# Cross-attention block: row sums of two units turned together, second exchange targets, and a changed order of work

## The chip, the cores and the metric

The kernel runs on one core of a Trainium2 chip. The metric is device time in microseconds (us), the median of several runs. A core has five engines with queues of their own: TensorE (PE, matrix products and transposes through the array), VectorE (DVE), ScalarE (ACT), GpSimd (POOL) and SyncE (SP, here only a queue that issues DMAs). Each engine works through its instructions in the order in which the program emits them, and waits where an operand or a buffer isn't ready.

## The reference

For four batches of 512 rows of width 512 (16 heads of 32):

```python
x = layer_norm(hidden_states, ln1_w, ln1_b)
q, k, v = x @ q_w + q_b, enc @ k_w + k_b, enc @ v_w + v_b     # split into heads
attn = softmax(where(mask, q @ k.T * scale, min))
hidden = (attn @ v) @ cproj_w + cproj_b + hidden_states
y = layer_norm(hidden, ln2_w, ln2_b)
y = gelu(y @ fc_w + fc_b)                                     # width 2048
return hidden + y @ proj_w + proj_b
```

All is float32.

## The kernel before

**Units and pairs.** Heads go in groups of four: w = 4 * batch + group, 16 in all. Each w has four units qt of 128 queries; unit u = 4w + qt runs from 0 to 63. Two units make a pair, number 2w + half, 0 to 31.

`scores` (L198) makes on PE the scores of one unit for four heads into one PSUM tile `sc`, of which there is a single buffer. DVE then adds the mask and finds each row's extreme (L210), and ACT takes the exponent and the row sum (L214), head by head. `turn` (L218) has to bring the 128 x 512 exponents of each head to a layout with keys on the partitions. For pairs 0, 3 and 6 (`ON_PE`) PE transposes them (`tpp`, L228) and DVE and ACT copy them out. For all others DVE transposes blocks of 32 x 32 into a tile `tb` (L242), and when the pair's second unit is done, 16 DMAs on SP's queue exchange the partition blocks from `tb` to a tile `pT` (L257). `tb` has two buffers, `pT` one. Two instructions of DVE in each unit bring the reciprocals of the row sums along: a reciprocal that is spread over 32 columns for each head (L245, `rrq`) and a transpose into the end of `tb` (L246). For a pair turned by PE, `over_sums` (L260) makes the spread reciprocals `rr` of both units at once, and `turn_sums` (L269) turns them on PE into `rb`.

`attend` (L279) multiplies a pair's turned exponents with v on PE (`av`, L299); DVE multiplies by the reciprocals into `oT` (L304), which is the last reader of `pT`. `cproj` (L323), `ln2` (L331), `ln2_turn`, `fc` (L355) and `proj` (L371) follow when a batch's eight pairs are done. `fc` writes gelu values to `gT`, four chunks for each quarter of the MLP, two buffers; `proj` reads them. The inputs of the projections are `encT` (L127) and `xT` (L149), one buffer each: encoder rows and normed rows, both with features on the partitions. `load_hid` (L315) fetches the residual and has POOL add a bias row; `ln2` norms each tile of it on DVE (L106) and has POOL add the MLP's output bias (L340), and `proj` adds its sums to it.

**Order.** Nothing is scheduled by a tool; each engine's order is the order of the calls. The main loop (L496) takes the units in turn: `scores`, then `attend` of the pair that is LAG = 4 units back (at even u, pair (u - 4) / 2), then `turn`. Between them it works off the list `first[w]`, and from qt = 2 on also `later[w]`, each item with a cost: 3.4 for a chain of PE, 0.5 for a set of four transposes, 0 for what doesn't use PE. A quarter of the sum is due in each unit, half of it before `turn` and half after (L513 to L519), and an item is taken while half its cost fits the budget (L423).

The lists are filled by hand (L457 to L493). A(w) loads the next weights and makes k, q and v; x1 to x4 load, take the statistics of, norm, turn and load the inputs of the next batch; C are the cproj chains, t2 the four turns of ln2, FC and PJ the chains of `fc` and `proj`, lo and hi the loads of the residual. For batch b at w = 4b:

```python
later[w] = C(p)
first[w + 1] = do(lambda: ln2(p))
first[w] = [load, ka] + x2[:1] + [qa] + x2[1:2] + p3[:1] + lo + x2[2:] + p3[1:3] + x3[:2] + [va] + x3[2:] + x4 + hi
first[w + 1] += [load, qa, ka] + t2[:2] + [va] + t2[2:] + p3[3:]
```

where p is the batch before. The last four items of PJ, FC and so on come after the loop (L522 on), with `attend` of pairs 30 and 31 between them.

Of the kernel before, what the change touches and what calls it, by code (L numbers as in the profile page):

```python
# [26 lines left out]
F32 = mybir.dt.float32  # L27
# [19 lines left out]
NW = B * NG  # L47
AHEAD = 3
LAG = 4
ON_PE = (0, 3, 6)  # L50
WARM = 14
PW = 2 * NT * HG * HD
# [7 lines left out]
def xattn_block(ctx: ExitStack, tc: tile.TileContext, x, encT, mask, q_w, k_w, v_w, c_w, fc_w, p_w, vecs, rows, out):  # L60
# [19 lines left out]
    nhalf = const.tile([P, NT], F32, tag="nhalf", name="nhalf")  # L80
    qb = const.tile([P, NG], F32, tag="qb", name="qb")
    wc = const.tile([P, ND, D], F32, tag="wc", name="wc")

    S = {}

# [37 lines left out]
    def queue(b):  # L123
        return nc.gpsimd if b else nc.sync

    def load_enc(b):
        S["eT", b] = one.tile([P, ND, L], F32, tag="encT", name=f"encT_{b}")  # L127
        for d in range(ND):
            queue(b).dma_start(out=S["eT", b][:, d, :], in_=encT[b, ts(d, P), :])

    def load_x(b):
        S["xn", b] = [tiles.tile([P, D], F32, tag="xn", name=f"xn1_{b}_{t}") for t in range(NT)]
# [12 lines left out]
            ln_rs((1, b))  # L145

    def ln1_turn(b, d):
        if d == 0:
            S["xT", b] = one.tile([P, ND, L], F32, tag="xT", name=f"xT_{b}")  # L149
        ln_turn((1, b), d, S["xn", b], S["xT", b])  # L150

    def make_mb(b):
        mb = one.tile([P, L], F32, tag="mb", name=f"mb_{b}")
# [11 lines left out]
    def prep_k(w):  # L165
        b, g = divmod(w, NG)
        kT = kqp.tile([P, L], F32, tag="kT", name=f"kT_{w}")
        acc = acc_tile(f"acck_{w}")
        for d in range(ND):
            nc.tensor.matmul(acc, S["wk", w][:, d, :], S["eT", b][:, d, :], start=(d == 0), stop=(d == ND - 1))  # L170
        nc.scalar.activation(kT, acc, AF.Identity, bias=vec[:, KB + g : KB + g + 1], scale=1.0)
        S["kT", w] = kT

    def prep_q(w):
        b, g = divmod(w, NG)
        qT = kqp.tile([P, L], F32, tag="qT", name=f"qT_{w}")
        acc = acc_tile(f"accq_{w}")
        for d in range(ND):
            nc.tensor.matmul(acc, S["wq", w][:, d, :], S["xT", b][:, d, :], start=(d == 0), stop=(d == ND - 1))  # L179

        nc.scalar.activation(qT, acc, AF.Identity, bias=qb[:, g : g + 1], scale=-scale)
        S["qT", w] = qT

    def prep_v(w):
        b = w // NG
        v = five.tile([P, NT, P], F32, tag="v", name=f"v_{w}")
        acc = acc_tile(f"accv_{w}")
        for t in range(NT):
            for d in range(ND):
                nc.tensor.matmul(  # L190
                    acc[:, ts(t, P)], S["eT", b][:, d, ts(t, P)], S["wv", w][:, d, :],
                    start=(d == 0), stop=(d == ND - 1),
                )
        nc.scalar.copy(v, acc.rearrange("p (t f) -> p t f", t=NT))
        S["v", w] = v
# [22 lines left out]
    def turn(w, qt):  # L218

        half, q = divmod(qt, 2)  # L220
        if 2 * w + half in ON_PE:
            if q == 0:

                S["pT", w, half] = two.tile([P, 2, NT, HG, P], F32, tag="tb", name=f"pT_{w}_{half}")
            for h in range(HG):
                tp = acc_tile(f"tpp_{w}_{qt}_{h}")
                for t in range(NT):
                    nc.tensor.transpose(tp[:, ts(t, P)], S["ps", w, qt][h][:, ts(t, P)], ident)  # L228
                o = S["pT", w, half][:, q, :, h, :]
                if h % 2:  # L230
                    nc.vector.tensor_copy(o, tp.rearrange("p (t q) -> p t q", t=NT))
                else:
                    nc.scalar.copy(o, tp.rearrange("p (t q) -> p t q", t=NT))
            return
        if q == 0:


            S["tb", w, half] = two.tile([P, NI, PW + 2 * HD], F32, tag="tb", name=f"tb_{w}_{half}")
        tb = S["tb", w, half]
        tv = tb[:, :, :PW].rearrange("p j (a t h q) -> p a h t j q", a=2, t=NT, h=HG)  # L240
        for h in range(HG):
            nc.vector.transpose(tv[:, q, h], S["ps", w, qt][h])  # L242

        rr = two.tile([P, HG, HD], F32, tag="rrq", name=f"rrq_{w}_{qt}")
        nc.vector.reciprocal(rr, S["sums", w][:, qt, :, None].broadcast_to([P, HG, HD]))  # L245
        nc.vector.transpose(tb[:, :, PW + q * HD : PW + (q + 1) * HD], rr.rearrange("p h d -> p (h d)"))  # L246
        if q == 0:
            return

        pT = one.tile([P, NI, PW + 2 * HD], F32, tag="pT", name=f"pT_{w}_{half}")  # L250

        for d in range(NI):
            for i in (0, 2, 1, 3):
                j = (i + d) % NI

                q = nc.scalar if w == NW - 1 and half and i % 2 else nc.sync
                q.dma_start(out=pT[ts(j, HD), i], in_=tb[ts(i, HD), j])  # L257
        S["pT", w, half] = pT

    def over_sums(w, half):  # L260

        if 2 * w + half not in ON_PE:
            return
        rr = one.tile([P, 2 * HG, HD], F32, tag="rr", name=f"rr_{w}_{half}")
        sums = S["sums", w][:, 2 * half : 2 * half + 2, :].rearrange("p t h -> p (t h)")
        nc.vector.reciprocal(rr, sums[:, :, None].broadcast_to([P, 2 * HG, HD]))
        S["rr", w, half] = rr.rearrange("p a d -> p (a d)")

    def turn_sums(w, half):  # L269
        if 2 * w + half not in ON_PE:  # L270
# [60 lines left out]
    def ln2(b):  # L331
        for f in range(FQ - 1):
            load_fc(b, f)
        ln_rs((2, b))
        S["yn", b] = [tiles.tile([P, D], F32, tag="xn", name=f"xn2_{b}_{t}") for t in range(NT)]
        for t in range(NT):
            h = S["hid", b, t]
            ln_norm((2, b), t, S["yn", b][t], h)

            nc.gpsimd.tensor_tensor(h, h, row[:, 1, :], ALU.add)  # L340

    def ln2_turn(b, d):
# [12 lines left out]
    def fc(b, f):  # L355
        q, k = divmod(f, FQ)

        if f + FQ - 1 < NF:
            load_fc(b, f + FQ - 1)
        if k == 0:  # L360
            S["gT", b, q] = two.tile([P, FQ, L], F32, tag="gT", name=f"gT_{b}_{q}")
        acc = acc_tile(f"accf_{b}_{f}")
        for d in range(ND):
            nc.tensor.matmul(acc, S["fw", b, f][:, d, :], S["yT", b][:, d, :], start=(d == 0), stop=(d == ND - 1))  # L364
        nc.scalar.activation(  # L365
            S["gT", b, q][:, k, :], acc, AF.Gelu_apprx_tanh, bias=vec[:, FCB + f : FCB + f + 1], scale=1.0
        )
        if q == 0:
            load_p(b, f)

    def proj(b, q, t):  # L371
        acc = acc_tile(f"accp_{b}_{q}_{t}")
        for k in range(FQ):
            nc.tensor.matmul(  # L374
                acc, S["gT", b, q][:, k, ts(t, P)], S["pw", b, q * FQ + k], start=(k == 0), stop=(k == FQ - 1)
            )
        h = S["hid", b, t]
        nc.vector.tensor_tensor(h, acc, h, ALU.add)  # L378
        if q == NQ - 1:
            nc.sync.dma_start(out=out[b, ts(t, P), :], in_=h)  # L380
        elif t == NT - 1:
            for k in range(FQ):
                load_p(b, (q + 1) * FQ + k)
# [5 lines left out]
    def do(fn):  # L389
        return [(0.0, fn)]  # L390
# [76 lines left out]
    for b in range(1, B):  # L467
        w = b * NG
        p = b - 1
        x1, x2, x3, x4 = inputs(b + 1) if b + 1 < B else ([], [], [], [])  # L470
        lo, hi = (do(lambda p=p, r=r: load_hid(p, r)) for r in ((0, 1), (2, 3)))
        p3 = PJ(b - 2, 3) if b > 1 else []
        t2 = turns2(p)
        first[w - (1 if b == 1 else 2)] += x1
        if b > 1:
            first[w - 1] += lo
            lo = []
        load, ka, qa, va = A(w + AHEAD)
        later[w] = C(p)
        first[w + 1] = do(lambda p=p: ln2(p))  # L480
        if b + 1 < B:
            first[w] = [load, ka] + x2[:1] + [qa] + x2[1:2] + p3[:1] + lo + x2[2:] + p3[1:3] + x3[:2] + [va] + x3[2:] + x4 + hi
            load, ka, qa, va = A(w + 1 + AHEAD)
            first[w + 1] += [load, qa, ka] + t2[:2] + [va] + t2[2:] + p3[3:]
        else:
            first[w] = [load, ka] + p3[:2] + hi
            first[w + 1] += [qa, p3[2]] + t2[:2] + [p3[3]] + t2[2:] + [va]
        first[w + 1] += FC(p, 0) + FC(p, 1)
        first[w + 2] = A(w + 2 + AHEAD) + PJ(p, 0) + FC(p, 2)
        f3 = FC(p, 3)  # L490
        first[w + 3] = A(w + 3 + AHEAD) + PJ(p, 1) + f3[:2]
        if b + 1 < B:
            first[w + 3] += PJ(p, 2) + f3[2:]  # L493

    nc.gpsimd.dma_start(out=wc, in_=c_w)
    for w in range(NW):  # L496
# [4 lines left out]
        due = 0.0  # L501
        for qt in range(NT):
            u = w * NT + qt
            at = divmod((u - LAG) // 2, 2) if u >= LAG and u % 2 == 0 else None
            if at:
                turn_sums(*at)
            scores(w, qt)
            if at:
                attend(*at)

            if qt == 2:
                work, rest = work + rest, []
# [20 lines left out]
    run(C(b))  # L533
    ln2(b)
    run(p3[2:])
    run(turns2(b))
    f3 = FC(b, 3)
    run(FC(b, 0) + FC(b, 1) + PJ(b, 0) + FC(b, 2) + PJ(b, 1) + f3[:2] + PJ(b, 2) + f3[2:] + PJ(b, 3))

# [43 lines left out]
```

## Time and profile before

| | |
|---|---|
| Time, median of 3 runs | 888.35 us (887.52 to 892.28) |
| The profiled run's own time | 889.65 us |
| Span of its instructions | 887.9 us |
| PE, busy | 849.1 us, 96% |
| DVE, busy | 511.6 us, 58% |
| ACT, busy | 337.1 us, 38% |
| POOL, busy | 167.4 us, 19% |
| Mean granted clock of TensorE | 0.983 |
| Exchanges pT<-tb | 456 DMAs on SP and 8 on ACT, 136 KB each, 2.5 us to landing |

A row of the groups reads: line, engine, operation, what it writes and reads, shape, number | busy us, mean ns of one | idle time of the engine just before, and what ended it. A line of the timeline reads: start in us, length in us, engine, line, operation, number in brackets after x, and in square brackets the idle time before it and who ended it. The granted clock is the share of its full rate that TensorE was given in a stretch. Durations come from the profiled run, the median from all runs.

### The profile page before, as it was taken

Reading aid. Unit: us, or ns where it says so; the run is one execution under the profiler, and the core shown is the slowest. Engines: PE = TensorE matmul, PEld = TensorE weight load, DVE = VectorE, ACT = ScalarE, POOL = GpSimd, SP = SyncE. Lnnn points to the kernel's source line nnn. Section 1 sums busy time; section 2 is a strip of 40 time slices with the busy share of each in tenths; the row PEclk is TensorE's granted clock in tenths of the full one; section 3 lists DMA queues with packets and bytes.
Section 4 is the critical chain, followed back from the end, with each engine's and each line's share of the span. In section 5 each row is a group of like instructions: output and inputs, shape, how many; then the busy total and the mean of one; then the engine's idle time right before and its main releaser. Section 6 shows DMA issues by size and latency. Waiting matters only on the chain.

```text
span 887.9 us, 10985 instructions
## 1 busy us (share of the span) xinstructions
PE 849.1 (96%) x3722; PEld 407.2 (46%) x3722; DVE 511.6 (58%) x1105; ACT 337.1 (38%) x699; POOL 167.4 (19%) x269
## 2 busy tenths in 40 slices
PE   9977979799999999999999999999999989999998
PEld 6535536445454544455454454435444334444443
DVE  3697757888547455778556635698567841501111
ACT  2646335334643434434453525424546320020000
POOL 2211001234101211224111110223101102521110
PEclk9998889899999999999999999999999999999999
DMA  7356265576854926566763835665757674232121
GB/s 262 107 134 171 66 152 147 134 207 161 207 149 109 264 67 172 156 175 181 203 167 79 220 98 125 165 188 148 199 123 194 153 172 144 83 118 82 43 80 56
DMA packets 43832, 130.14 MB, mean 147 GB/s; under 512 B 11456, under 2 KB 11456, under 8 KB 43648
## 3 DMA queue, kind: packets, MB, share of 16 engines
q1 hardware_dynamic: 26064, 71.40, 32.6%
q0 software_dynamic: 17184, 56.90, 21.5%
q10 hardware_dynamic: 528, 1.14, 0.6%
q8 instruction: 30, 0.49, 0.2%
q14 instruction: 26, 0.21, 0.1%
HBM read 60.58 MB, written 4.19 MB: 73 GB/s over the span
## 4 chain that ended last, share of the span: by engine, by line
PE 77%; DVE 8%; DMA 8%; SPq 4%; issue 1%; ACT 1%; POOL 0%; DVEq 0%; ACTq 0%
PE accp L374 23%; PE accf L364 21%; DMA pT<-tb 7%; PE av L299 6%; PE accv L190 6%; PE accq L179 6%; PE sc L205 5%; PE acck L170 5%; SPq L257 4%; DVE s L210 3%; PE accc L326 3%; DVE tb L242 2%; PE tp L115 2%; DMA encT<-encT_dram 1%; PE tpp L228 1%
## 5 line engine op out<-in xcount | busy, mean ns | idle before, releaser
L214 ACT ACTIVATE s<-s,mn 128x512 f32<-128x512 f32 x256 | 181.6, 710 | 165.5 <-DVE mn L210 165.3
L364 PE MATMUL accf<-yT,fw 128*128 128x512 f32 x512 | 225.8, 595 | 1.8 <-ACT yT L120 1.8
L374 PE MATMUL accp<-pw,gT 128*128 128x512 f32 x512 | 226.9, 596 | 0.0
L210 DVE CUSTOM_DVE_ANT_0 s<-sc,mb 128x512 f32<-128x512 f32 x256 | 161.0, 685 | 104.2 <-PE sc L205 104.0
L378 DVE TENSOR_TENSOR hid<-accp,hid 128x512 f32<-128x512 f32 x64 | 43.8, 686 | 192.8 <-PE accp L374 192.8
L364 PEld LDWEIGHTS accf<-yT,fw 128*128 128x128 f32 x512 | 95.9, 190 | 124.7 <-issue 118.3
L374 PEld LDWEIGHTS accp<-pw,gT 128*128 128x128 f32 x512 | 95.6, 190 | 122.9 <-issue 119.1
L242 DVE STREAM_TRANSPOSE tb<-s 128x512 f32<-128x512 f32 x232 | 148.7, 685 | 2.7 <-ACT s L214 2.3
L365 ACT ACTIVATE gT<-accf,vec 128x512 f32<-128x512 f32 x64 | 44.0, 687 | 192.9 <-PE accf L364 175.8
L353 POOL DMA_DIRECT2D pw<-p_w_dram x64 | 34.3, 536 | 284.3 <-PE accp L374 284.3
L299 PE MATMUL av<-pT,v 128*32 128x256 f32 x1024 | 68.3, 411 | 18.8 <-DMA pT<-tb 13.4
L205 PE MATMUL sc<-kT,qT 32*128 32x512 f32 x512 | 73.9, 647 | 6.0 <-DVE mn L210 5.1
L190 PEld LDWEIGHTS accv<-wv,encT 128*128 128x128 f32 x512 | 59.7, 194 | 6.7 <-issue 3.7
L299 PEld LDWEIGHTS av<-pT,v 128*32 128x32 f32 x1024 | 33.5, 116 | 62.7 <-issue 28.5
L190 PE MATMUL accv<-wv,encT 128*128 128x128 f32 x512 | 61.3, 279 | 0.0
L349 POOL DMA_DIRECT2D fw<-fc_w_dram x64 | 34.5, 540 | 142.0 <-PE accf L364 133.9
L170 PE MATMUL acck<-encT,wk 128*128 128x512 f32 x128 | 59.4, 603 | 0.7 <-DMA encT<-encT_dram 0.7
L179 PE MATMUL accq<-xT,wq 128*128 128x512 f32 x128 | 59.8, 610 | 0.0
L326 PE MATMUL accc<-wc,oT 128*128 128x512 f32 x128 | 56.6, 596 | 0.0
L245 DVE RECIPROCAL rrq<-sums 128x128 f32<-128x128 f32 x58 | 52.7, 909 | 0.0
L214 ACT ACTIVATION_READ_ACCUMULATOR s<-s,mn 128x1 f32 x256 | 47.7, 187 | 0.0
L214 ACT ACT_TABLE_LOAD x21 | 26.9, 1283 | 37.0 <-DVE mn L210 37.0
(58 smaller groups left out, 486.9 us busy)
## 6 DMA issues: line engine op xcount, KB each, us to landing
pT<-tb SPq DMA_DIRECT2D x456, 136.0 KB, 2.5
fw<-fc_w_dram POOLq DMA_DIRECT2D x64, 256.0 KB, 3.7
pw<-p_w_dram POOLq DMA_DIRECT2D x64, 256.0 KB, 3.5
hid<-x_dram POOLq DMA_DIRECT2D x16, 256.0 KB, 4.3
out_dram<-hid SPq DMA_DIRECT2D x16, 256.0 KB, 2.0
wk<-k_w_dram POOLq DMA_DIRECT2D x15, 256.0 KB, 4.9
wq<-q_w_dram POOLq DMA_DIRECT2D x15, 256.0 KB, 4.6
wv<-v_w_dram POOLq DMA_DIRECT2D x15, 256.0 KB, 5.1
```

The costliest lines, as they stand in the source:

```text
L170: nc.tensor.matmul(acc, S["wk", w][:, d, :], S["eT", b][:, d, :], start=(d == 0), stop=(d == ND - 1))
L179: nc.tensor.matmul(acc, S["wq", w][:, d, :], S["xT", b][:, d, :], start=(d == 0), stop=(d == ND - 1))
L190: nc.tensor.matmul(acc[:, ts(t, P)], S["eT", b][:, d, ts(t, P)], S["wv", w][:, d, :], start=(d == 0), stop=(d == ND - 1),)
L205: nc.tensor.matmul(sc[:, h, :], qT[r, ts(qt, P)], kT[r, :], start=True, stop=True)
L210: nc.vector.tensor_tensor_reduce(out=s, in0=sc[:, h, :], in1=S["mb", w // NG], scale=1.0, scalar=FMAX, op0=ALU.add, op1=ALU.min, accum_out=mn,
L214: nc.scalar.activation(s, s, AF.Exp, bias=mn, scale=-1.0, accum_out=sums[:, qt, h : h + 1])
L242: nc.vector.transpose(tv[:, q, h], S["ps", w, qt][h])
L245: nc.vector.reciprocal(rr, S["sums", w][:, qt, :, None].broadcast_to([P, HG, HD]))
L299: nc.tensor.matmul(av[ts(h, HD), : 2 * P].rearrange(shape, **kw), v[:, t, ts(h, HD)], p[t][h], start=(t == 0), stop=(t == NT - 1),)
L326: nc.tensor.matmul(acc, S["oT", b][:, g, ts(t, P)], wc[:, g, :], start=(g == 0), stop=(g == NG - 1))
L364: nc.tensor.matmul(acc, S["fw", b, f][:, d, :], S["yT", b][:, d, :], start=(d == 0), stop=(d == ND - 1))
L374: nc.tensor.matmul(acc, S["gT", b, q][:, k, ts(t, P)], S["pw", b, q * FQ + k], start=(k == 0), stop=(k == FQ - 1))
```

## The change

- **Row sums.** In a pair that is turned by DVE, the reciprocals of both units are taken together after the second unit: a reciprocal of the 128 x 8 sums, a copy that spreads it to 128 x 256 (`rr`), and one transpose. `over_sums` is split in the same way. `rr` has one buffer for both uses.
- **Exchange targets.** The MLP's tile becomes a fixed tile `gt` with the two halves of gT in it, and the projections' inputs a fixed tile `xe` with eT and xT in it. Pairs 2 and 5 exchange into `gt`, pairs 29 and 31 into `xe`, all others into `pT` as before.
- **Later attends.** Pairs 1, 2, 4 and 5 are attended at units 7, 9, 13 and 15 (before 6, 8, 12 and 14).
- **Batch two's order.** In `first[4]` and `later[4]` the statistics of the next batch's inputs stand ahead of the q chain, the norms ahead of the v chain, two of the turns after it and two behind the first cproj chain, and the loads of the residual come after the encoder's.
- **ln2's turns.** Three of the four, instead of two, come before the v chain, for batches 0 and 1.
- **Proj bias.** The four adds on POOL leave `ln2` and are emitted after the turns.

```diff
+IN_G = (2, 5)
+IN_XE = (29, 31)
+AT = {7: 1, 9: 2, 13: 4, 15: 5}
...
+    xe = const.tile([P, NI * (PW + 2 * HD)], F32, tag="xe", name="xe")
+    gt = const.tile([P, NI * (PW + 2 * HD)], F32, tag="gt", name="gt")
+    eT, xT = (xe[:, i * ND * L : (i + 1) * ND * L].rearrange("p (d l) -> p d l", d=ND) for i in range(2))
+    gT = [gt[:, i * FQ * L : (i + 1) * FQ * L].rearrange("p (k l) -> p k l", k=FQ) for i in range(2)]
...
-        rr = two.tile([P, HG, HD], F32, tag="rrq", name=f"rrq_{w}_{qt}")
-        nc.vector.reciprocal(rr, S["sums", w][:, qt, :, None].broadcast_to([P, HG, HD]))
-        nc.vector.transpose(tb[:, :, PW + q * HD : PW + (q + 1) * HD], rr.rearrange("p h d -> p (h d)"))
         if q == 0:
             return
 
-        pT = one.tile([P, NI, PW + 2 * HD], F32, tag="pT", name=f"pT_{w}_{half}")
+        rs = small.tile([P, 2, HG], F32, tag="rsum", name=f"rsum_{w}_{half}")
+        nc.vector.reciprocal(rs, S["sums", w][:, 2 * half : 2 * half + 2, :])
+        rr = one.tile([P, 2, HG, HD], F32, tag="rr", name=f"rr_{w}_{half}")
+        nc.vector.tensor_copy(rr, rs[:, :, :, None].broadcast_to([P, 2, HG, HD]))
+        nc.vector.transpose(
+            tb[:, :, PW:].rearrange("p j (a q) -> p a j q", a=2), rr.rearrange("p a h d -> p (a h d)")
+        )
+
+        pair = 2 * w + half
+        if pair in IN_G or pair in IN_XE:
+            pT = (gt if pair in IN_G else xe).rearrange("p (i n) -> p i n", i=NI)
+        else:
+            pT = one.tile([P, NI, PW + 2 * HD], F32, tag="pT", name=f"pT_{w}_{half}")
...
+    def proj_bias(b):
+        for t in range(NT):
+            h = S["hid", b, t]
             nc.gpsimd.tensor_tensor(h, h, row[:, 1, :], ALU.add)
...
+        bias = do(lambda p=p: proj_bias(p))
+        if b == 1:
+            first[w] = [load, ka] + x2[:2] + [qa] + x2[2:] + [va] + x3[:2] + x4 + lo + hi
+            later[w] = later[w][:1] + x3[2:] + later[w][1:]
+        elif b + 1 < B:
+            first[w] = [load, ka] + x2[:1] + [qa] + x2[1:2] + p3[:1] + x2[2:] + p3[1:3]
+            first[w] += x3[:2] + [va] + x3[2:] + x4 + hi
         if b + 1 < B:
-            first[w] = [load, ka] + x2[:1] + [qa] + x2[1:2] + p3[:1] + lo + x2[2:] + p3[1:3] + x3[:2] + [va] + x3[2:] + x4 + hi
             load, ka, qa, va = A(w + 1 + AHEAD)
-            first[w + 1] += [load, qa, ka] + t2[:2] + [va] + t2[2:] + p3[3:]
+            first[w + 1] += [load, qa, ka] + t2[:3] + [va] + t2[3:] + bias + p3[3:]
         else:
             first[w] = [load, ka] + p3[:2] + hi
-            first[w + 1] += [qa, p3[2]] + t2[:2] + [p3[3]] + t2[2:] + [va]
+            first[w + 1] += [qa, p3[2]] + t2[:2] + [p3[3]] + t2[2:] + bias + [va]
...
-            at = divmod((u - LAG) // 2, 2) if u >= LAG and u % 2 == 0 else None
-            if at:
-                turn_sums(*at)
+            pair = AT.get(u, (u - LAG) // 2 if u >= LAG and u % 2 == 0 else None)
+            if pair in AT.values() and u not in AT:
+                pair = None
+            if pair is not None:
+                turn_sums(*divmod(pair, 2))
             scores(w, qt)
-            if at:
-                attend(*at)
+            if pair is not None:
+                attend(*divmod(pair, 2))
```

More of the change, by code (lines that the diff above doesn't have):

```diff
@@ L126, in load_enc @@
     def load_enc(b):
-        S["eT", b] = one.tile([P, ND, L], F32, tag="encT", name=f"encT_{b}")
         for d in range(ND):
-            queue(b).dma_start(out=S["eT", b][:, d, :], in_=encT[b, ts(d, P), :])
+            queue(b).dma_start(out=eT[:, d, :], in_=encT[b, ts(d, P), :])
     def load_x(b):
@@ L147, in ln1_turn @@
     def ln1_turn(b, d):
-        if d == 0:
-            S["xT", b] = one.tile([P, ND, L], F32, tag="xT", name=f"xT_{b}")
-        ln_turn((1, b), d, S["xn", b], S["xT", b])
+        ln_turn((1, b), d, S["xn", b], xT)
     def make_mb(b):
@@ L169, in prep_k @@
         for d in range(ND):
-            nc.tensor.matmul(acc, S["wk", w][:, d, :], S["eT", b][:, d, :], start=(d == 0), stop=(d == ND - 1))
+            nc.tensor.matmul(acc, S["wk", w][:, d, :], eT[:, d, :], start=(d == 0), stop=(d == ND - 1))
         nc.scalar.activation(kT, acc, AF.Identity, bias=vec[:, KB + g : KB + g + 1], scale=1.0)
@@ L178, in prep_q @@
         for d in range(ND):
-            nc.tensor.matmul(acc, S["wq", w][:, d, :], S["xT", b][:, d, :], start=(d == 0), stop=(d == ND - 1))
+            nc.tensor.matmul(acc, S["wq", w][:, d, :], xT[:, d, :], start=(d == 0), stop=(d == ND - 1))
         nc.scalar.activation(qT, acc, AF.Identity, bias=qb[:, g : g + 1], scale=-scale)
@@ L190, in prep_v @@
                 nc.tensor.matmul(
-                    acc[:, ts(t, P)], S["eT", b][:, d, ts(t, P)], S["wv", w][:, d, :],
+                    acc[:, ts(t, P)], eT[:, d, ts(t, P)], S["wv", w][:, d, :],
                     start=(d == 0), stop=(d == ND - 1),
@@ L263, in over_sums @@
             return
[L264 to L267, printed above, removed]
+        rs = small.tile([P, 2, HG], F32, tag="rsum", name=f"rsum_{w}_{half}")
+        nc.vector.reciprocal(rs, S["sums", w][:, 2 * half : 2 * half + 2, :])
+        rr = one.tile([P, 2, HG, HD], F32, tag="rr", name=f"rr_{w}_{half}")
+        nc.vector.tensor_copy(rr, rs[:, :, :, None].broadcast_to([P, 2, HG, HD]))
+        S["rr", w, half] = rr.rearrange("p a h d -> p (a h d)")
     def turn_sums(w, half):
@@ L359, in fc @@
             load_fc(b, f + FQ - 1)
-        if k == 0:
-            S["gT", b, q] = two.tile([P, FQ, L], F32, tag="gT", name=f"gT_{b}_{q}")
         acc = acc_tile(f"accf_{b}_{f}")
@@ L365, in fc @@
         nc.scalar.activation(
-            S["gT", b, q][:, k, :], acc, AF.Gelu_apprx_tanh, bias=vec[:, FCB + f : FCB + f + 1], scale=1.0
+            gT[q % 2][:, k, :], acc, AF.Gelu_apprx_tanh, bias=vec[:, FCB + f : FCB + f + 1], scale=1.0
         )
@@ L374, in proj @@
             nc.tensor.matmul(
-                acc, S["gT", b, q][:, k, ts(t, P)], S["pw", b, q * FQ + k], start=(k == 0), stop=(k == FQ - 1)
+                acc, gT[q % 2][:, k, ts(t, P)], S["pw", b, q * FQ + k], start=(k == 0), stop=(k == FQ - 1)
             )
@@ L535, in xattn_block @@
     run(p3[2:])
-    run(turns2(b))
+    run(turns2(b) + do(lambda: proj_bias(b)))
     f3 = FC(b, 3)
```

## The prediction

> **What bounds the kernel now.** Read first is the busy row of each engine, then the slices with the granted clock, then the waits of PE, then the timeline at each of them.
>
> ```profile
> PE 849.1 (96%) x3722; PEld 407.2 (46%) x3722; DVE 511.6 (58%) x1105; ACT 337.1 (38%) x699; POOL 167.4 (19%) x269
> ...
> PEclk9998889899999999999999999999999999999999
> ```
>
> TensorE is busy 96% of 887.9 us, so a change that leaves its work alone (this one does) can win only PE's idle time and slow clock. The gaps over 0.25 us between matmuls sum to 33.3 us. The waits of PE name them:
>
> ```profile
> PE av L299 <- DMA pT<-tb: 13.4, 7, 4.5
> PE tp L115 <- DVE xn L106: 6.3, 1, 6.3
> PE av L299 <- ACT s L214: 5.1, 1, 5.1
> PE sc L205 <- DVE mn L210: 5.1, 2, 4.0
> PE accf L364 <- ACT yT L120: 1.8, 1, 1.8
> ```
>
> The timeline places them (start, length, instruction, idle before it):
>
> ```profile
> 48.12 1.14 PE L205 MATMUL sc<-kT,qT 32*128 32x512 f32 x8 [1.02 <-DVE mn L210]
> ...
> 63.63 2.09 PE L205 MATMUL sc<-kT,qT 32*128 32x512 f32 x8 [4.04 <-DVE mn L210]
> ...
> 88.58 3.64 PE L299 MATMUL av<-pT,v 128*32 128x256 f32 x32 [4.46 <-DMA pT<-tb]
> ...
> 122.30 3.64 PE L299 MATMUL av<-pT,v 128*32 128x256 f32 x32 [5.10 <-ACT s L214]
> ...
> 171.10 2.61 PE L115 MATMUL tp<-ident,xn 128*128 128x128 f32 x8 [6.35 <-DVE xn L106]
> ...
> 722.08 3.20 PE L299 MATMUL av<-pT,v 128*32 128x256 f32 x32 [3.42 <-DMA pT<-tb]
> ```
>
> The fourth blames ACT, whose exponents had ended; the exchange of pair 4 landed at 121.86, so it is the DMA. An undisturbed `av` row is 1.93 long, here 3.64: windows of 2 us show a granted clock of 0.50 for 6.8 us after each of the four gaps of 4 to 6.4 us, and for 3.4 us after 718. Half the stretch in which PE works at half clock is lost: 2.9, 2.3, 2.55, 2.05 and 1.3, in all 11.1 us. What there is to win is thus about 44 us. A unit u is 4w+qt; units 0 to 16 start at 24, 31, 37, 42, 48, 55, 64, 76, 83, 96, 105, 111, 116, 132, 142, 149, 154.
>
> **Row sums.** The rows of before:
>
> ```profile
> L245 DVE RECIPROCAL rrq<-sums 128x128 f32<-128x128 f32 x58 | 52.7, 909 | 0.0
> L246 DVE STREAM_TRANSPOSE tb<-rrq 128x128 f32<-128x128 f32 x58 | 18.1, 312 | 2.0
> L266 DVE RECIPROCAL rr<-sums 128x256 f32<-128x256 f32 x3 | 5.2, 1742 | 0.0
> ```
>
> Two units cost 2 x (0.909+0.312) = 2.44 us. The two reciprocals give 6.5 ns an element and 0.08 fixed, so one over 8 elements is 0.13. The copy of 256 elements lies between 0.27 (half of L106's 0.54 for 512 from SBUF) and 0.42 (L304, 256 from PSUM); the transpose of 256 near 0.41, between 0.31 and 0.60. With the waits between dependent steps I take 0.9 to 1.0 a pair: 1.45 less, all 1.2 of the even unit and 0.25 of the odd one. Times 29 that is 42 us, and 1.15 each for the three pairs turned by PE. From unit 20 on DVE waits for PE (104 us before scoring), so there it is worth nothing; it counts where DVE is full, in 40 to 70.
>
> A wait is added: `rr` is one buffer, which PE's `turn_sums` of pairs 3 and 6 read at units 10 and 16, and the copies of pairs 4 and 7 now wait for that. Behind them on DVE stands one 0.41 transpose and then scoring, which waits for the same PE anyway: at most 0.5 us on the exchange's start, nothing on PE. Without that cover 0.5 each.
>
> **Units 3 to 16, re-timed by hand from the rows.** DVE: the over-sums at 37.9 shrink by 1.15, unit 2's sums by 1.2, so scoring of unit 4 starts at 49.3, not 51.6, and the 1.02 gap goes. Unit 5's scoring ends at 60.2 (63.5 before); PE is there at 58.55, so 4.04 becomes 1.65. Pair 2's target is `gt`, free, so its exchange starts at 63.6 instead of 71.75 (after `oT` of pair 1). Exchanges took 11.8 to 20 us from first issue to last landing, these 16.5: landed by 80; attended now at unit 9, on PE at 86.6. The 4.46 goes. Pair 4's starts at 96.5 (105.44), took 16.4: 113; attended at unit 13, at 115. The 5.10 goes. Pair 5's follows it in SP's queue from 109.5 and lands near 125, needed at 132. Gone: 1.02 + 2.4 + 4.46 + 5.10 = 13.0, and the clock's 7.75.
>
> Given back: the attends that leave units 6 and 12 were PE's filler there. In unit 6 DVE has four norms (1.9) and the sums ahead of scoring; scoring ends at 68.0, the last exponent at 69.1. PE, through with `accq` at 64.9 and without `av`, waits at its `tpp`, whose fourth buffer is freed by `qT` behind the exponents: scores of unit 7 at 71.4 where the work alone gives 67.6, 3.8 lost in pieces of up to 2.1. In unit 12 the same costs 0.8. Sum: 20.7 - 4.6 = **16.1**.
>
> Here the Trainium skill's "TensorE: Matmul & The Clock Gate", Part 1, bears: the clock halves after an idle window of about 3.4 us and returns after one busy window. By the rows the half clock lasts two such windows (6.8) after gaps of 4 and more; gaps of 1.66 and 1.77 left it at 1.00. By the rule's return, five episodes would cost 8.5 us, by the rows 11.1; I take the rows. Pieces under 2.1 should keep it by both; else 2.9 is lost again.
>
> **Batch two.** Before, PE reached the turns of batch 2 right after unit 17's scores, while DVE had four statistics, scoring and POOL's root ahead. Now `accv` (3.6) lies before them and the statistics come a half unit earlier: all xn are normed 15.5 us after unit 16's start, where PE ends `accv` at 14.9: with the hand-over about 0.9 left of 6.35 + 2.05: **7.5**. What this moves: `load_hid` on POOL behind four encoder loads (4 x 0.54, and `accv`'s end) and its adds (1.27 each) behind the landing; the first is ready at most 1.6 late for `cproj`'s DVE add. DVE stalls, behind it two turns and unit 19's scoring, for which PE has 2.7 to spare. Nothing, then; otherwise up to 2. The other turns fall between cproj chains and lengthen the stretch from `oT` of pair 7 to attend 8, an exchange of 15.6 with 0.79 of wait: plus or minus 1, taken as nothing.
>
> **Turns of ln2, proj bias.** With three turns before `accv`, only the DVE one is late for `accf`; its chunk comes last, 2.6 after the first. Of the 1.77 gap 1.3 stays won, 0.5 lost to the third turn waiting for a norm. The bias seems to free DVE:
>
> ```profile
> L106 DVE TENSOR_SCALAR xn<-hid,mv,rs 128x512 f32<-128x512 f32 x16 | 15.2, 1014 | 1.4 <-POOL rs L102 1.4
> ...
> L106 DVE TENSOR_SCALAR xn<-xn,mv,rs 128x512 f32<-128x512 f32 x16 | 7.6, 538 | 2.9 <-POOL rs L102 2.9
> ```
>
> Two norms of each batch last 1.49 because POOL's adds run beside them. The skill's "SBUF — State Buffer", Who interferes with whom, calls the port pair of DVE and GpSimd an exclusive lock: whoever starts later blocks fully. By the rule apart from them 1.9 us a batch would be saved. But POOL doesn't follow PE's order: in its queue only three weight loads (3 x 0.54) come between the root and the adds, none for batch 3 and the tail, and these start when the first norm ends, as now. So 0, at most 1.9 a batch on a DVE that has slack; the weight loads start 5.6 earlier, the adds are done long before `accp`. The same lock speaks against the new copies: 32 times some 0.3 us in which POOL may wait, hidden by its 81% idle; at worst 10 us of POOL.
>
> **The end.** Pair 29 waited for `oT` of 28 (689.0, its rows ready at 684.9), pair 30 for `oT` of 29 (705.84, ready at 702.4, now 701.1). With `xe` for 29 and 31 they go when ready: 30 lands at 701.1 + 15.9 = 717, PE asks at 717.9. Gone: 0.78 + 3.42 + 1.3 = **5.5**. The last readers of `encT` and `xT` are the chains that w = 13 issues, so `xe` is free. The gaps of 0.91, 1.66, 0.33 and 1.35 at 296, 501, 578 and 597 stay: their exchange starts at an `oT` that follows PE at once, and lasts 12 to 20.
>
> **Sum.** 16.1 + 7.5 + 1.3 + 5.5 = 30.4. The profiled run took 889.65 (span 887.9), the median is 888.35: 888.35 - 30.4 = **858.0**.
>
> **Rivals.** (a) More is hidden: unit 6 loses 1, the mid gaps halve: 5 to 8 more, about 851. For: my DVE steps are rounded upward. Against: the order in unit 6 is fixed. 17%. (b) Less: unit 6 and 12 cost the clock (2 x 2.9), attend 8 waits 2, hid 2, pair 4's landing holds the source buffer that unit 12's copies need (113 against 112; 3 if it takes 20): 868. For: exchange times spread. 25%. (c) Slower. `gt` holds both halves of the MLP's tile, `xe` both inputs. If readers wait by the whole tile, each `accp` chain begins only after the last gelu of the other half, which in the loop ends 1.4 to 4 us after PE: three crossings in each of three batches at 4, three at 1 in the tail: 39, above 30.4: 897. It decides from 3 us a crossing on. Against it: `accf` ran four records at 214.27 while chunks 2 and 3 of the same yT were written at 215.9 to 217.9, so waits go by region. 5%. (d) It doesn't do what it says: attends still wait since exchanges only lengthen beside each other; 888. Against: from 64 to 71 and from 89 to 105 no exchange ran. 2%. My forecast 51%.
>
> The range for eight in ten reaches from (a) to (b): 848 to 871. About 0.5% can be told from no change: faster 0.93, same 0.02, slower 0.05.
>
> **What would show it.** Right: no PE wait over 3 us after 30, clock rows of 1.00 but for the ends, pair 2's exchange issued near 64, a wait of some 2 at `tpp` of unit 6, L106 still with 1.49 rows, the pair's sums under 1.0. Wrong: waits of `accp` for gelu, half clock in 65 to 72, attends 4 or 5 still waiting, or a copy over 0.5.

## The result, and the profile after

The changed kernel took **860.5 us** (median of 4 runs, 858.69 to 861.97), the kernel before, on the same chip, 888.13 (887.52 to 892.28): a ratio of 0.9678, with a 95% interval of 0.9644 to 0.9713. Predicted were 858.0. The profiled run took 861.97 with a span of 860.2, so by the spans 27.7 us went, where the sum had 30.4.

Busy row and granted clock of the changed kernel:

```profile
PE 839.3 (98%) x3722; PEld 403.3 (47%) x3722; DVE 466.5 (54%) x1079; ACT 337.0 (39%) x699; POOL 167.3 (19%) x269
...
PEclk9999999999999999999999999999999999999999
```

PE does the same 3722 matmuls in 9.8 us less of busy time, and the mean granted clock is 1.000 in place of 0.983: the half clock, reckoned at 11.1, is gone from this execution. DVE is 45 us less busy, where 42 plus 3 x 1.15 had been reckoned. What PE still waits for, in the same view as before:

```profile
PE av L314 <- DMA pT<-tb: 5.2, 3, 2.4
PE av L314 <- DMA xe<-tb: 3.1, 1, 3.1
PE tpp L234 <- ACT s L220: 1.8, 1, 1.8
PE sc L211 <- DVE mn L216: 1.6, 1, 1.6
...
PE tpp L234 <- ACT qT L187: 1.1, 2, 0.6
```

The wait of 6.3 for the norms is gone. The waits of `av` for exchanges, 13.4 and 5.1 before, are down to 5.2 and 3.1, and those of `sc` for DVE from 5.1 to 1.6. The longest single wait is now at the end. The timeline of PE places them:

```profile
60.21 1.14 PE L211 MATMUL sc<-kT,qT 32*128 32x512 f32 x8 [1.64 <-DVE mn L216]
66.81 2.07 PE L234 MATMUL tpp<-ident,s 128*128 128x128 f32 x12 [1.83 <-ACT s L220]
69.50 0.66 PE L234 MATMUL tpp<-ident,s 128*128 128x128 f32 x4 [0.62 <-ACT qT L187]
71.00 1.14 PE L211 MATMUL sc<-kT,qT 32*128 32x512 f32 x8
...
176.17 1.93 PE L314 MATMUL av<-pT,v 128*32 128x256 f32 x32 [2.38 <-DMA pT<-tb]
...
695.67 1.93 PE L314 MATMUL av<-pT,v 128*32 128x256 f32 x32 [3.12 <-DMA xe<-tb]
```

The first four rows are unit 6 as it was re-timed by hand: the scores wait 1.64 (predicted 1.65), then `tpp` waits in two pieces, and the scores of unit 7 come at 71.00 (71.4). The `av` rows last 1.93, so the clock was whole. The last two rows are what the prediction had at about nothing: attend 8 and the attend at the end. (The last row's label names `xe`, but it is pair 30's exchange into `pT` that landed last before it, at 695.37.) The gaps over 0.25 us between matmuls add up to 15.5 us, against 33.3 before.

The groups of DVE that carry the row sums, and the norms of the residual:

```profile
L253 DVE RECIPROCAL rsum<-sums 128x8 f32<-128x8 f32 x29 | 4.6, 160 | 0.0
L255 DVE COPY rr<-rsum 128x256 f32<-128x256 f32 x29 | 8.5, 294 | 1.8 <-PE tpr L289 0.8
L256 DVE STREAM_TRANSPOSE tb<-rr 128x256 f32<-128x256 f32 x29 | 12.9, 445 | 1.0
...
L115 DVE TENSOR_SCALAR xn<-hid,mv,rs 128x512 f32<-128x512 f32 x16 | 15.4, 1021 | 1.4 <-POOL rs L111 1.4
```

A pair's sums cost 0.16 + 0.29 + 0.45 = 0.90 us, where two units cost 2.44. The copy waited for PE's `turn_sums` for 0.8 us in all, the added wait. The mean norm is still 1021 ns: the moved bias did nothing to it.

### The profile page after: what moved, and what is told of

The parts are those of the page before. It is cut to its first block, busy times and chain, and to the rows that moved or that the text cites. A ratio compares the mean times of both kernels' runs of the same rounds, so it can differ in the third digit from the quotient of the medians.

```text
span 860.2 us, 10987 instructions
## 1 busy us (share of the span) xinstructions
PE 839.3 (98%) x3722; PEld 403.3 (47%) x3722; DVE 466.5 (54%) x1079; ACT 337.0 (39%) x699; POOL 167.3 (19%) x269
## 4 chain that ended last, share of the span: by engine, by line
PE 82%; DVE 7%; DMA 7%; SPq 3%; issue 1%; ACT 0%; DVEq 0%; ACTq 0%
PE accp L390 24%; PE accf L380 23%; PE accv L196 6%; PE av L314 6%; PE sc L211 6%; PE accq L185 5%; PE acck L176 5%; DMA pT<-tb 5%; PE accc L341 3%; DVE s L216 3%; DVE tb L248 2%; SPq L271 2%; PE tp L124 1%; PE tpp L234 1%; DMA xe<-encT_dram 1%
## 5 line engine op out<-in xcount | busy, mean ns | idle before, releaser
L390 PE MATMUL accp<-pw,gt 128*128 128x512 f32 x512 | 226.9, 596 | 0.0
L390 PEld LDWEIGHTS accp<-pw,gt 128*128 128x128 f32 x512 | 95.8, 190 | 122.7 <-issue 118.8
L381 ACT ACTIVATE gt<-accf,vec 128x512 f32<-128x512 f32 x64 | 44.0, 687 | 194.3 <-PE accf L380 187.5
L314 PE MATMUL av<-pT,v 128*32 128x256 f32 x896 | 54.2, 382 | 9.2 <-DMA pT<-tb 5.2
L196 PEld LDWEIGHTS accv<-wv,xe 128*128 128x128 f32 x512 | 58.8, 192 | 7.1 <-issue 3.4
L196 PE MATMUL accv<-wv,xe 128*128 128x128 f32 x512 | 60.7, 277 | 0.0
L176 PE MATMUL acck<-xe,wk 128*128 128x512 f32 x128 | 59.3, 603 | 0.9 <-DMA xe<-encT_dram 0.9
L185 PE MATMUL accq<-xe,wq 128*128 128x512 f32 x128 | 58.5, 600 | 0.0
L314 PEld LDWEIGHTS av<-pT,v 128*32 128x32 f32 x896 | 27.5, 110 | 44.1 <-issue 18.3
L211 PEld LDWEIGHTS sc<-kT,qT 32*128 32x128 f32 x512 | 20.0, 183 | 41.4 <-issue 28.8
```

The costliest lines, as they stand in the source:

```text
L176: nc.tensor.matmul(acc, S["wk", w][:, d, :], eT[:, d, :], start=(d == 0), stop=(d == ND - 1))
L185: nc.tensor.matmul(acc, S["wq", w][:, d, :], xT[:, d, :], start=(d == 0), stop=(d == ND - 1))
L196: nc.tensor.matmul(acc[:, ts(t, P)], eT[:, d, ts(t, P)], S["wv", w][:, d, :], start=(d == 0), stop=(d == ND - 1),)
L211: nc.tensor.matmul(sc[:, h, :], qT[r, ts(qt, P)], kT[r, :], start=True, stop=True)
L314: nc.tensor.matmul(av[ts(h, HD), : 2 * P].rearrange(shape, **kw), v[:, t, ts(h, HD)], p[t][h], start=(t == 0), stop=(t == NT - 1),)
L381: nc.scalar.activation(gT[q % 2][:, k, :], acc, AF.Gelu_apprx_tanh, bias=vec[:, FCB + f : FCB + f + 1], scale=1.0)
```

## The experiments

The theory: time comes from DVE's row sums and from exchanges that start earlier and are attended later, which together open units 4 to 13 and with them the clock; batch two's order takes away the norm's wait; the bias does nothing. The rivals: one of the parts does all; the parts only move the waits; the remaining 2.7 us of the sum lie in the clock, in attend 8 or at the end. Medians and ratios, each to the kernel before in its own job (its median 894.01, 889.86 and 891.29 in the three jobs, so ratios are compared, not medians); the span is that of one profiled run:

| kernel | median us | ratio, 95% | span |
|---|---|---|---|
| changed kernel | 860.5 | 0.9678 [0.9644, 0.9713] | 860.2 |
| before, with the new row sums alone | 882.27 | 0.9877 [0.9826, 0.9927] | 878.0 |
| changed, old row sums | 865.88 | 0.9709 [0.9672, 0.9745] | 867.5 |
| changed, no `gt`, old attends | 875.63 | 0.9806 [0.976, 0.9852] | 869.4 |
| changed, old attends | 869.59 | 0.9767 [0.9709, 0.9824] | 865.5 |
| changed, old order of batch two | 867.22 | 0.971 [0.9672, 0.9749] | 869.2 |
| changed, bias behind `fc` | 860.84 | 0.9688 [0.9627, 0.9749] | 858.6 |
| changed, no `xe` | 861.85 | 0.9677 [0.9632, 0.9722] | 862.5 |
| changed, pair 31 all on SP | 858.48 | 0.9652 [0.9585, 0.9719] | 864.1 |
| changed, pair 8 into `gt` | 858.35 | 0.9633 [0.9609, 0.9658] | 855.6 |
| changed, pair 1 at unit 6 | 863.57 | 0.9684 [0.9652, 0.9717] | 861.6 |
| pair 8 into `gt` and 31 on SP | 857.63 | 0.9617 [0.959, 0.9645] | 856.2 |
| the last three together | 856.47 | 0.9611 [0.9583, 0.9639] | 853.3 |

Whole runs scatter by several us, and most of the intervals overlap. A finer measure is the time between two fixed marks on PE, the scores of one unit and those of a later one. From unit 0 to unit 16 it is 112.87 or 112.88 us in all five kernels that share the changed order there and kept the full clock, so parts of the change can be sized by it (us, one profiled run each; an asterisk marks a stretch with half clock in it):

| kernel | units 0 to 16 | 16 to 20 | 20 to 22 |
|---|---|---|---|
| before | 129.44* | 43.35* | 26.30 |
| changed kernel | 112.87 | 35.33 | 25.90 |
| before, with the new row sums alone | 123.16* | 43.32* | 26.01 |
| changed, old row sums | 117.14* | 36.21 | 29.99* |
| changed, no `gt`, old attends | 122.98* | 35.33 | 24.13 |
| changed, old attends | 117.73* | 35.33 | 26.18 |
| changed, old order of batch two | 114.05* | 43.70* | 23.45 |
| changed, pair 8 into `gt` | 112.88 | 35.33 | 23.92 |
| changed, pair 1 at unit 6 | 111.51* | 35.33 | 27.45* |
| the last three together | 111.02 | 35.33 | 23.46 |

### The row sums alone, and undone

The kernel before with only the edit of `turn` and `over_sums`; and the changed kernel with the reciprocals as before:

```diff
-        rs = small.tile([P, 2, HG], F32, tag="rsum", name=f"rsum_{w}_{half}")
-        nc.vector.reciprocal(rs, S["sums", w][:, 2 * half : 2 * half + 2, :])
...
+        rr = two.tile([P, HG, HD], F32, tag="rrq", name=f"rrq_{w}_{qt}")
+        nc.vector.reciprocal(rr, S["sums", w][:, qt, :, None].broadcast_to([P, HG, HD]))
```

> The kernel before with the new row sums only. My theory: the sums are worth something only where DVE is full, in units 3 to 5: the wait of 1.02 goes, 4.04 becomes 1.65 without half clock behind it; the exchanges of pairs 2 and 4 still start at oT of the pair before and keep PE waiting with half clock, batch two's 6.35 stays. About 881 us (878 to 885). Rival, that DVE's 45 us of saved work is what made the kernel faster: 860 to 868. Rival, that targets and order did it: 887.

> The changed kernel with the old row sums in each unit. My theory: the waits of units 4 and 6 before the scores come back (1 and 4, with 2.9 of half clock), unit 12's transposes and batch two's norms come 1 later: about 869 us (866 to 873). If DVE's saved work made the gain: 880 or more. If only targets and order did: 861.

Alone, the sums give 1.2% of the 3.2%. PE's waits with the sums alone:

```profile
PE av L304 <- DMA pT<-tb: 11.9, 8, 4.6
PE tp L115 <- DVE xn L106: 6.3, 1, 6.3
PE av L304 <- ACT s L214: 4.3, 1, 4.3
PE accf L369 <- ACT yT L120: 1.8, 1, 1.8
PE sc L205 <- DVE mn L210: 1.6, 1, 1.6
```

Against before, the waits of `sc` fell from 5.1 to 1.6 (the 1.02 and the 4.04 to 1.64 that the prediction gave to DVE). The waits of `av` at pairs 2 and 4 hardly changed, from 4.46 to 4.59 and from 5.10 to 4.32; the norm's 6.3 and the 1.8 of `accf` are as they were. So a faster DVE alone makes the rows ready sooner, but PE waits as long for the exchanges, which begin when `pT` comes free. With the old sums in the changed kernel the reverse is seen:

```profile
PE av L309 <- DMA pT<-tb: 9.3, 4, 4.5
PE sc L211 <- DVE mn L216: 5.1, 2, 4.0
```

The 1.01 and 4.04 before `sc` are back, and attend 8 waits 4.50. By the span that costs 7.3 us; by the ratios it is 0.3%, within both intervals. The first piece put in gives 9.9 us of span, the same piece taken out costs 7.3; up to unit 16 it gives 6.3 and costs 4.3. The parts overlap, and no share of the whole belongs to one of them.

### The targets and the later attends

```diff
-IN_G = (2, 5)
-AT = {7: 1, 9: 2, 13: 4, 15: 5}
+IN_G = ()
+AT = {}
```

and, as the last of these, only `AT = {}` with the targets kept.

> The changed kernel with pairs 2 and 5 exchanged into pT and the attends at their old units. My theory: pair 2's and 4's exchanges wait for oT again, two waits of 4 to 5 with 2.5 of half clock each come back, less the 4.6 that the missing fillers cost in units 6 and 12, plus a wait of 1.8 for pair 1: about 871 us (867 to 875). If the later attends only moved the waits: 861. The last pairs are as in the changed kernel.

> The changed kernel with all attends at their old units, targets as changed. My theory: pair 1 waits 1.8 in unit 6 but fills it, pair 2 and 5 have landed, pair 4 lands about 4 after PE asks, with half clock behind it: about 864 us (861 to 868). If the targets alone are enough and the later attends only took the fillers away: 857.

Without both, 1.3% is lost, and the interval is apart from that of the changed kernel. Its timeline, in two places:

```profile
84.44 1.94 PE L314 MATMUL av<-pT,v 128*32 128x256 f32 x16 [4.81 <-DMA pT<-tb]
```

```profile
116.79 3.26 PE L314 MATMUL av<-pT,v 128*32 128x256 f32 x32 [3.87 <-DMA pT<-tb]
```

The waits at pairs 2 and 4 are back, and with them rows of half clock (16 matmuls in 1.94 where 32 took 1.93). With the targets kept and only the attends early, pair 4 is asked for before its exchange has landed (110.9):

```profile
111.23 3.64 PE L314 MATMUL av<-pT,v 128*32 128x256 f32 x32 [5.42 <-DMA gt<-tb]
```

So the targets start exchanges early, but pair 4's own still goes to `pT` and takes 16.7 us here (15.4 in the changed kernel); only the later attend gives it that time. By the stretch from unit 0 to 16, putting the old attends back costs 4.9 us, and taking `gt` away from pairs 2 and 5 as well another 5.3. The later attends without the targets were not run.

### Batch two's order as before

```diff
-        if b == 1:
-            first[w] = [load, ka] + x2[:2] + [qa] + x2[2:] + [va] + x3[:2] + x4 + lo + hi
-            later[w] = later[w][:1] + x3[2:] + later[w][1:]
-        elif b + 1 < B:
-            first[w] = [load, ka] + x2[:1] + [qa] + x2[1:2] + p3[:1] + x2[2:] + p3[1:3]
+        if b + 1 < B:
+            first[w] = [load, ka] + x2[:1] + [qa] + x2[1:2] + p3[:1] + lo + x2[2:] + p3[1:3]
```

> The changed kernel with the old order of work in batch two (w = 4). My theory: the 6.35 before the turns comes back with 2.05 of half clock, and the wait before attend 8 falls from 2.4 to about 0.8: 866 to 868 us. If the faster sums had removed that wait anyway: 861.

```profile
155.42 2.60 PE L124 MATMUL tp<-ident,xn 128*128 128x128 f32 x8 [6.35 <-DVE xn L115]
```

The same 6.35 as before, with the turns at half clock (2.60, in the changed kernel 1.65), and no wait at attend 8. From unit 16 to 20 the old order costs 8.4 us, and from 20 to 22 it gives 2.5 back, mainly the wait at attend 8: 5.9 in all. The span is 9.0 us longer, but this execution also fell to half clock three times (at 68, 580 and 703 us) where the order is the same. By the ratios it is 0.3%, which the intervals don't separate. Every run of it took longer than every run of the changed kernel (866.3 to 870.98 against 858.69 to 861.97), but its job's runs of the kernel before were longer too.

### The bias where it could help

In the changed kernel the bias follows `ln2` in POOL's own queue with little between. Here it is emitted behind two chains of `fc`, whose weight loads wait on PE:

```diff
-            first[w + 1] += [load, qa, ka] + t2[:3] + [va] + t2[3:] + bias + p3[3:]
-        first[w + 1] += FC(p, 0) + FC(p, 1)
+            first[w + 1] += [load, qa, ka] + t2[:3] + [va] + t2[3:] + p3[3:]
+        first[w + 1] += FC(p, 0)[:2] + bias + FC(p, 0)[2:] + FC(p, 1)
```

> The changed kernel with the bias adds emitted behind the second fc chain, whose weight load waits for PE, so that POOL really comes to them later. My theory: the norms that took 1.49 beside the adds fall to 0.54 (1.9 a batch less on DVE), and the time stays within 1 us of 860.5, since DVE has slack there. If the lock cost time: up to 7.6 less, 853.

```profile
L115 DVE TENSOR_SCALAR xn<-hid,mv,rs 128x512 f32<-128x512 f32 x16 | 7.9, 555 | 1.4 <-POOL rs L111 1.4
...
L115 DVE TENSOR_SCALAR xn<-xn,mv,rs 128x512 f32<-128x512 f32 x16 | 7.6, 540 | 1.4 <-POOL rs L111 1.4
```

Now the norms of `hid` cost what those of `xn` cost: the adds on POOL were what lengthened them, by 7.5 us in all. The time is the same (0.9688), since DVE has slack there. Both halves of the prediction's 0 hold: the move doesn't part them, and parting them is worth nothing that can be told.

### The end

First without the two targets at the end (`IN_XE = ()`), then with all of pair 31's DMAs on SP's queue:

```diff
-                q = nc.scalar if w == NW - 1 and half and i % 2 else nc.sync
+                q = nc.sync
```

> The changed kernel with pairs 29 and 31 exchanged into pT. My theory: the waits before attends 29 and 30 come back as 0.8 and 3.4 with 1.3 of half clock, in place of 3.1: about 863 us. If the end's targets gave nothing: 860.5.

> The changed kernel with all of pair 31's exchange on SP's queue, behind pair 30's. Theory one, that pair 31's halves on ACT's queue hold up pair 30's last two pieces: the wait of 3.1 before attend 30 falls to 1 to 1.7, 859 us. Theory two, that the MLP's weight loads made that exchange 19.6 long: 3 stays, 860.5.

Without `xe` the waits are 1.65 and 2.36 in place of one of 3.12, and the ratio is the same: as they stand, the targets at the end are worth nothing that can be measured. With all on SP the wait before attend 30 is gone (0.2); so it is in the two later kernels that do the same (0 and 0.68), while it is 1.5 to 3.1 in every kernel that has `xe` and keeps the split. The ratio alone, 0.9652, doesn't separate it from the changed kernel. The stretch from the scores of unit 63 to the end does: 176.1 to 176.8 us in the three kernels with all on SP, 177.7 to 180.0 in the eight with `xe` and the split, 180.2 without `xe` (the three of 179.9 and more had 3.4 us of half clock in it).

Why: SP's timeline of the changed kernel, then of the kernel with pair 8 in `gt` and 31 on SP.

```profile
675.79 16.22 SPq L271 DMA_DIRECT2D pT<-tb  x16
692.12 7.11 SPq L271 DMA_DIRECT2D xe<-tb  x6
```

```profile
674.98 10.64 SPq L271 DMA_DIRECT2D pT<-tb  x16
689.08 10.32 SPq L271 DMA_DIRECT2D xe<-tb  x16
```

To issue pair 30's 16 DMAs SP needs 16.2 us in one and 10.6 in the other. The delays begin before ACT issues anything (its first DMA is at 689.87), so they aren't traffic of ACT's queue. The semaphore events of the trace show what they are. The exchanges' DMAs of SP and ACT signal their landing on eight semaphores in rotation, and one is issued only when the DMA that had its semaphore before has landed. Pair 31 with a target of its own waits for no reader of `pT`, and in the rotation its ACT half now stands among pair 30's last DMAs and takes every other place. The last five of pair 30 in the changed kernel (us from the start, semaphores numbered 0 to 7):

```
DMA     semaphore  issued   landed   earlier user of the semaphore landed
12th    2          682.72   690.98   680.63 (5th)
13th    4          684.87   691.25   684.85 (7th)
14th    6          687.57   691.58   687.55 (9th)
15th    0          690.61   693.64   690.60 (11th)
16th    2          691.16   695.37   690.98 (12th)
```

Each of the last four is issued as soon as that landing is in. With all on SP the five use semaphores 1 to 5 in turn, whose earlier users are the 4th to the 8th, and they are issued from 681.92 to 685.02. Without `xe` they use 1 to 5 as well, and so they do in the kernel before: there pair 31 waits for `pT` and stands behind. A DMA of this exchange took up to 8.5 us to land (the MLP's weight loads, issued from 678.71 to 682.02, run beside it), so a few places in the rotation matter. It is the two together, `xe` for pair 31 and its split over two queues, that make pair 30 last 17.3 to 19.6 us in the eight kernels that have both; without `xe` it lasted 16.3 (the sums alone) and 16.7, with all on SP 16.3 to 17.1, before 15.9. That leaves part of the 3.7 us over 15.9 to other causes.

### Attend 8, unit 6, and what is left

Pair 8 takes `gt` too (`IN_G = (2, 5, 8)`); pair 1 is attended at 6 again (`AT` without `7: 1`); then pair 8 with pair 31 on SP, and all three.

> The changed kernel with pair 8 exchanged into gt as well, which is free until the first gelu of unit 21. Theory: the 2.4 before attend 8 is the exchange starting at oT of pair 7 (159.7) where its rows are ready at 156.2; it starts 3.5 earlier and the wait goes: about 858 us. If it is made long by the encoder's and the residual's loads beside it, the wait shrinks little: 860.

> The changed kernel with pair 1 attended at unit 6 again. Theory, that the later attend took unit 6's filler: PE waits up to 1.8 for the landing, but the two waits at tpp (1.83 and 0.62) go, and unit 7 starts its v chain some 1.5 earlier: 859 us. If unit 6 is bound by DVE either way: 860.5.

> Pair 8 in gt and all of pair 31's exchange on SP. The waits before attends 8 and 30 (2.4 and 3.1) both go or nearly: about 855.5 us, 2.4 and 2.6 off 860.5.

> Pair 8 in gt, all of pair 31's exchange on SP, pair 1 attended at unit 6. If the three add up: about 854 us, and with fewer broken stretches of PE fewer runs with half clock.

PE at attend 8 with pair 8 in `gt`:

```profile
172.29 1.14 PE L211 MATMUL sc<-kT,qT 32*128 32x512 f32 x8
173.36 1.93 PE L314 MATMUL av<-gt,v 128*32 128x256 f32 x32
```

No idle time: the exchange ran from 155.88 to 170.46, no longer from `oT` of pair 7 on (159.67 to 175.82). PE in unit 6 with pair 1 attended there:

```profile
59.79 1.14 PE L211 MATMUL sc<-kT,qT 32*128 32x512 f32 x8 [1.64 <-DVE mn L216]
61.31 3.41 PE L314 MATMUL av<-pT,v 128*32 128x256 f32 x32 [0.38 <-DMA pT<-tb]
...
71.07 1.14 PE L211 MATMUL sc<-kT,qT 32*128 32x512 f32 x8
```

The filler closes the gap before `tpp`, and yet the scores of unit 7 come at 71.07, against 71.00. With the clock whole they don't come sooner either: 10.8 us after unit 6's in the last kernel as in the changed one, so what sets that time isn't PE's work. But unit 7 no longer holds the attend, and unit 8 comes sooner: up to unit 16 the stretch is 111.02 us with pair 1 at unit 6 and a whole clock, against 112.87. So of the about 3.3 us that unit 6 gives back (its scores to unit 7's take 10.8 where PE's work alone needs 7.5) this filler wins 1.9. In the kernel with this edit alone a part of it was lost again, since `av` ran at half clock (3.41) after gaps of 1.64 and 0.38, and its whole runs, at mean clocks of 0.993 to 0.999, show no gain.

All three together are the fastest version, 0.9611 [0.9583, 0.9639], just below the interval of the changed kernel; its waits before attends 8 and 30 are 0 and 0.68. Whole runs don't tell it from the kernel without pair 1's move (0.9617). Pair 8's target is worth 2.0 to 2.4 us from unit 20 to 22 (23.46 to 23.92 in the three kernels that have it, 25.90 in the changed one).

## Why the prediction was right

The mechanism was right in each large part, and the size within 3 us of 30. By its own steps, from one profiled run each:

- **Row sums**: 0.9 to 1.0 a pair, measured 0.90; DVE 45 us less. The copy was 0.29, in the lower part of 0.27 to 0.42; the wait that was added was at most 0.5, as said, with nobody behind it on PE.
- **Units 3 to 16**: 16.1 against 16.3 (unit 16 starts at 137.31, before at 153.62; from unit 0 on 16.6, since this run started 0.27 later). The 1.02 is gone, 4.04 became 1.64; pair 2's exchange starts at 63.48 (63.6), pair 4's at 96.18 (96.5) and lands at 111.56 (113). Given back in unit 6: 3.8 predicted, about 3.3 measured, 2.45 of it as visible gaps; in unit 12 0.8 and 0.49. That these pieces kept the clock was in part luck: in two of the seven profiled executions with the same units 6 to 16 (the old order, pair 31 on SP) the gap of 1.83 or 1.84 was followed by 3.4 us of half clock, which made the stretch from unit 6 to 16 longer by 1.2 and 0.7.
- **Batch two**: 7.5 against 8.0 (unit 16 to the scores of unit 20: 43.35 before, 35.33 after).
- **Attend 8**: "plus or minus 1, taken as nothing" was mis-sized: the wait went from 0.79 to 2.38, a loss of 1.6. The other order makes PE reach it sooner, while its exchange still starts at `oT` of pair 7, at 159.67, although the rows were ready near 156.2. Giving the pair a target that is free removes the wait; with the old order it isn't there either.
- **Turns of ln2**: 1.3 against 2.0 (from the start of attend 8 to the scores of unit 22: 24.37 us before, 22.38 after). **Bias**: 0, and 0.
- **The gaps in the middle**: 4.25 in all before, 3.72 now, so 0.5 was won that wasn't counted.
- **The end**: this term was the worst. Of the 5.5, 2.4 came: 0.78 + 3.42 + 1.3 before, 3.12 after. The step that failed is "30 lands at 701.1 + 15.9 = 717". Pair 30 started in time, at 675.79, and PE asked 16.8 us later, so with a length of 15.9 there would have been no wait. It lasted 19.6, in good part since the target given to pair 31 put that pair's split DMAs among its own. The length was taken from an exchange that had no other behind it in the rotation.

Terms as measured: 16.3 + 8.0 - 1.6 + 2.0 + 2.4 + 0.5 = 27.6, of 27.7 by the spans. Rival (c) failed: there is no wait of `accp` for gelu among PE's waits, so `gt` and `xe` are waited for by region. Rival (b) named attend 8 with 2, and that happened; its other costs, the clock in units 6 and 12, did not in this run. The prediction's step "the half clock lasts two such windows (6.8) after gaps of 4 and more" held as an observation; the last section has what the traces show behind it.

**What stays open.** By the ratios each single part, the targets with their attends excepted, lies within the intervals when it is undone; the sizes above rest on stretches and waits in the trace of single executions. The turns of ln2 were never undone alone, nor the targets with the later attends kept. Of the 3.7 us by which pair 30's exchange became longer, a part has no cause shown.

## What to carry to other kernels

Where a buffer's last reader starts a transfer, ask what else is idle then and has the size: a second target made pairs 2, 5 and 8 start as soon as their rows were ready, but it paid in full only when the reader was put late enough for the transfer's whole length. A faster engine by itself (1.2%) moves the wait to the next release; look for what is released last before pricing the gain. Where whole runs scatter more than a part is worth, compare the time between two fixed marks on the busiest engine. When a transfer's length goes into a sum, read from the trace how long its issue takes and what each of its DMAs waits for, not only its mean from issue to landing.

## What the runs showed of the hardware that was not expected

- **DMAs in two queues are coupled by their completion semaphores** in this program: an exchange that is split over SP and ACT made the one before it longer once it no longer waited for that one's buffer: 17.3 to 19.6 us against 15.9 before and 16.3 to 17.1 with all on one queue, with issue times that follow landings by 0.01 to 0.2 us.
- **The clock changed on a grid, and a gap counted by where it fell in it.** The Trainium skill's "TensorE: Matmul & The Clock Gate", Part 1, puts the fall at an idle window of about 3.4 us. In the kernel with pair 1 at unit 6 it fell although PE was never idle for that long (length, then busy us of PE, PEld, DVE, ACT, POOL, then clock, DMA share, GB/s):

```profile
60.00:62.00 2.00, 1.62 (x20) 0.61 (x20) 2.00 (x4) 1.50 (x5) 0.36 (x1) 0.90 0.86 205
62.00:64.00 2.00, 2.00 (x25) 1.21 (x20) 1.93 (x7) 0.00 (x0) 0.00 (x0) 0.50 0.60 231
```

  In all 14 traces the changes of the granted clock within an execution lie whole multiples of 3.413 us apart, on a grid that begins at another moment in each execution. Some windows of that grid (us from the start of the span):

```
kernel                   window           PE busy  clock after it  gap of PE
pair 1 at unit 6          58.20 -  61.61   42%     0.50            1.64 and 0.38, both inside
pair 31 all on SP         63.60 -  67.02   45%     0.50            1.84, inside
changed                   62.93 -  66.34   60%     1.00            1.83, cut by the window's end
changed                   66.34 -  69.76   65%     1.00            the rest of it, and 0.62
changed                  690.99 - 694.40   46%     1.00            3.12, cut by the window's end
changed                  694.40 - 697.81   63%     1.00            the rest of it
before                   164.91 - 168.33    0%     0.50            6.35, the larger part
before                   168.33 - 171.74   19%     0.50            the rest of it
before                   171.74 - 175.15  100%     1.00            none
```

  Each of the 35 falls follows a window in which PE was busy for 50% or less. Under 42% the clock always fell; from 42 to 50% it fell 6 times and stayed 13 times (the shares are rough, since the ends of matmuls are modelled). So the length agrees with the page, but the window need not be idle. The clock came back after the first window with PE busy for 77% or more, and not after any of 72% or less: the 6.8 us after gaps of 4 and more are two windows, the first of which still held the rest of the gap. So the prediction's pieces under 2.1 were not safe: 1.84 was enough where it fell inside one window, and 3.12, split over two, was not. Which of the two happens differs between runs of one kernel: with pair 31 on SP, one run took 855.43 at a mean clock of 1.000 and another 865.86 at 0.991, of which the lower clock is an estimated 8 us (0.009 of 866). It isn't the only cause of scatter: two runs of the changed kernel, both at 1.000, took 858.69 and 861.97.
